# Layer 3 of a four-layer convolution net: who copies halo rows, how VectorE's side work begins and ends, and in which order pixels come back

## The chip, the core and the metric

The kernel runs on one core of a Trainium2 chip, in one launch. The metric is the device time in microseconds (us), as the median of several executions. The engines are named as in the profile: PE is TensorE's matmul, PEld its loading of weights, DVE is VectorE, ACT is ScalarE, POOL is GpSimd, and SP is the engine that issues most transfers.

## The reference

An input x of 4 images, 48 channels and 256 x 256 pixels, in f32, goes through four layers of the form x = x + f(groupnorm(x)). Layer 0 is a gated depthwise block with a frequency filter at its end; layers 1 and 2 are recurrent scans down, up, right and left through the image. Layer 3, the one that changes, computes this:

```python
y = einsum('oc,bchw->bohw', w_in, x)            # 48 -> 288 channels
yp = y in patches of 8 x 8
f = rfft2(yp) * fft_mask[None]                  # a real mask per channel and frequency
y = irfft2(f) put back as an image
y = depthwise 3 x 3 convolution(y, w_dw)        # padding 1
x1, x2 = split(y, 2, axis=1)                    # 144 channels each
g = gelu(x1) * x2
return einsum('oc,bchw->bohw', w_out, g)        # 144 -> 48 channels
```

## The kernel before

The four layers run one after the other. Layer 3 (line 716 on) handles the images in two pairs, and each pair in strips of 8 rows: 32 steps with rows and one short tail step that ends the last row, so 66 steps in all. A step is named (pair, strip) in the code.

**The stages of a step.** `fetch` (line 801) loads the raw rows through SP. `normed` (L818) applies the group norm on ScalarE, in four instructions, into `u`. `turned` transposes it (L830 on PE, copied by ACT in L834), and `waves` takes the patches to frequencies (L844, copied by ACT in L845 into `xf`, which shares its buffer with `u`). `spectrum` is run 16 times: TensorE mixes the channels (L855, tile `pz`), and VectorE multiplies by the mask on the way out of PSUM (L857 and L861). `pixels` brings one group of channels back to pixels, 16 matmuls (L886, tile `pp`) and two copies by ACT (L890), into a tile `z_` with two halo rows above and a halo column on either side.

**The five groups.** A pair has two images of 288 channels. The first 128 channels of x1 and of x2 are a0 and a1 for the first image and b0 and b1 for the second; the last 16 of each, for both images, are m, on 64 partitions. `order` lists them as a0, a1, b0, b1, m, and `back(step, k)` brings back group k.

**Who convolves.** TensorE convolves a0, a1 and m, with a diagonal 32 x 32 matrix for each of the nine taps (`taps`, L903, tile `pd`). Two generators, `lane(0)` and `lane(1)`, each own half of the array's rows; a tap of one lane is eight matmuls of the program. A lane takes m first where the strip's parity is its own, and then a0 and a1; at the end `gate` (L917, L918) applies gelu to x1 on ACT and multiplies by x2 on DVE, into the single buffers `g_a` and `g_m`. VectorE convolves b0 and b1 by itself (`side`, line 924): the first tap is an ACT instruction (L941) that starts an accumulator `acc`, in two halves of four rows; the eight other taps are 16 DVE instructions (L943). After b0's taps, ACT applies gelu to the whole accumulator (L947), and after b1's taps two DVE products (L950) end the unit.

**The end of a step.** `mixed` projects 144 channels to 48 on TensorE (L962 from VectorE's product, L971 from the gated buffers; tile `po`), adds the raw rows on DVE (L984), and issues the stores on SP (L991). It runs one step late: `store(steps[n - 1])` stands in step n. A lane may gate step n only when the store of step n - 1 has been put in the order.

**What sets the order.** The order of TensorE's and VectorE's instructions in this layer is the order in which the program is written out (a manual schedule for these two engines); ScalarE's and GpSimd's instructions are put in order by the framework's scheduler. `in_turns` (line 427) does the writing. It takes turns: each lane gives one tap; then pieces of `work()` (each a condition, a cost in us, an action) go out as the credit that the taps earn allows; then VectorE's `side` is advanced by as much time as has been spent, up to 4 us ahead. A piece whose condition isn't met holds up the pieces behind it. All PSUM tiles of this layer come from one pool of four.

**Halo rows.** Before a group's new pixels are written, the last two rows of the strip before are copied to rows 0 and 1 of the same tile: on GpSimd for a0, a1, b0 and b1 (L879), and on ScalarE for m (L877), whose two strips lie in different halves of the partitions.

## Time and profile before

| what | us |
|---|---|
| median of 3 executions (14871.17 to 14875.96) | 14873.32 |
| the profiled execution's own time | 14874.17 |
| its span, from the first to the last instruction | 14872.4 |
| PE busy in the span | 13297.2 (89%) |
| DVE busy | 7342.2 (49%) |
| ACT busy | 3320.0 (22%) |
| POOL busy | 2818.1 (19%) |
| layer 3, from its first to its last step's first spectrum | 9349 to 14757 |

The profile is of one execution. Its page gives the busy time of each engine, and the granted clock of TensorE in 40 slices. The trace answers with more: groups of instructions by line (count, busy time, mean length of one, the idle time before them and what ended it), the waits (who waited for whom: total, times, longest), the chain of work that ended last in order of time, the timeline, and windows (for a stretch of time: the busy time of PE, PEld, DVE, ACT and POOL with their instructions, the granted clock of TensorE, the share and the rate of the DMA). Times in the last two are counted from the span's start. Within layer 3 a tap of `L903` stands in the trace as 16 matmuls, two for each of the program's.

### The profile page before, as it was taken

To read this page: it belongs to the slowest core of one execution; us is meant where nothing else is said; L and a number is where in the kernel's file an instruction comes from. 1 tells how busy PE (TensorE), PEld (TensorE's weight loads), DVE (VectorE), ACT (ScalarE), POOL (GpSimd) and SP (SyncE) were. 2 spreads that over 40 slices of the span, in tenths; PEclk is the share of its full clock that TensorE was granted. 3 is DMA by queue.
4 is the path that set the end of the run, shared out by engine and by line. 5 is a ranking of instruction groups with operands and counts; after the bars stand their busy time and mean duration, and the time that the engine had idled before them with its cause. 6 is when DMAs were issued, how large, how long until landed. Compare 5 with 4: busy or idle time off the path is not lost.

```text
span 14872.4 us, 340743 instructions
## 1 busy us (share of the span) xinstructions
PE 13297.2 (89%) x155976; PEld 8329.4 (56%) x155976; DVE 7342.2 (49%) x13291; ACT 3320.0 (22%) x3110; POOL 2818.1 (19%) x1227
## 2 busy tenths in 40 slices
PE   3999999998999898889999978788888888888888
PEld 1444444445777676667767756444444444444444
DVE  5333333333333334433333445666666666666666
ACT  1222222222223000012330000233233323333322
POOL 0000000000000004410000144223222222322322
PEclk9999999999999999999999988899999989999999
DMA  7222222214755876767567676100100110011010
GB/s 161 48 52 47 49 51 47 49 46 95 153 136 155 159 151 165 183 139 148 144 157 157 133 186 158 28 19 19 23 19 19 23 19 19 19 23 19 19 23 17
DMA packets 1168810, 1219.21 MB, mean 82 GB/s; under 512 B 1025941, under 2 KB 1030541, under 8 KB 1106509
## 3 DMA queue, kind: packets, MB, share of 16 engines
q1 hardware_dynamic: 1069260, 649.62, 22.2%
q0 software_dynamic: 87488, 445.55, 10.7%
q10 hardware_dynamic: 10624, 102.24, 3.5%
q8 instruction: 1224, 20.05, 0.6%
q14 instruction: 214, 1.75, 0.0%
HBM read 699.84 MB, written 497.42 MB: 81 GB/s over the span
## 4 chain that ended last, share of the span: by engine, by line
PE 73%; DVE 15%; DMA 6%; ACT 2%; issue 2%; SPq 1%; POOL 1%; ACTq 0%; DVEq 0%; POOLq 0%
PE acc L502 32%; PE pd L270 13%; DVE acc L943 13%; PE pd L903 7%; PE pp L886 5%; PE pz L855 4%; PE ph L245 3%; DMA blk<-x 3%; PE po L971 2%; PE po L355 2%; PE po L962 2%; DMA x<-blk 1%; PE pf L333 1%; PE py L302 1%; DMA gx<-in_x 1%
## 5 line engine op out<-in xcount | busy, mean ns | idle before, releaser
L502 PE MATMUL acc<-line,w_down 96*96 96x256 f32 x12240 | 2650.5, 379 | 41.7 <-DMA in<-x 23.3
L943 DVE SCALAR_TENSOR_TENSOR acc<-z_b,wd,acc 128x1024 f32<-128x1024 f32 (+1 forms) x2080 | 2481.1, 1264 | 396.6 <-ACT acc L941 395.3
L502 PEld LDWEIGHTS acc<-line,w_down 96*96 96x96 f32 x12240 | 1996.0, 163 | 695.5 <-issue 42.4
L879 POOL COPY z_b<-z_b 128x512 f32<-128x512 f32 x128 | 1470.2, 11486 | 3096.1 <-DVE acc L943 3053.8
L886 PE MATMUL pp<-c_idft,z 128*128 128x128 f32 x10240 | 1374.7, 298 | 645.4 <-ACT xf L845 558.8
L886 PEld LDWEIGHTS pp<-c_idft,z 128*128 128x128 f32 x10240 | 1304.4, 194 | 925.9 <-ACT xf L845 613.4
L270 PE MATMUL pd<-main,diag 32*32 32x512 f32 x36864 | 1670.5, 599 | 32.8 <-issue 32.5
L903 PE MATMUL pd<-z_a,diag 32*32 32x512 f32 x37152 | 1589.0, 619 | 105.9 <-DVE g_m L918 93.9
L502 PE MATMUL acc<-line,w_left 96*96 96x256 f32 x6120 | 1362.7, 386 | 251.3 <-DVE line L685 251.3
L502 PE MATMUL acc<-line,w_right 96*96 96x256 f32 x6120 | 1335.1, 380 | 104.9 <-DVE line L646 40.9
L502 PEld LDWEIGHTS acc<-line,w_left 96*96 96x96 f32 x6120 | 1016.9, 166 | 596.7 <-DVE line L685 257.3
L502 PEld LDWEIGHTS acc<-line,w_right 96*96 96x96 f32 x6120 | 1002.1, 164 | 437.9 <-DVE line L646 42.8
L857 DVE TENSOR_TENSOR z<-pz,mask 128x512 f32<-128x512 f32 x1024 | 702.3, 686 | 590.3 <-PE pz L855 588.6
L270 PEld LDWEIGHTS pd<-main,diag 32*32 32x32 f32 x36864 | 594.2, 103 | 656.4 <-issue 536.4
L270 PE MATMUL pd<-rest,diag 32*32 32x512 f32 x18432 | 936.6, 597 | 22.9 <-issue 22.9
L646 DVE SCALAR_TENSOR_TENSOR line<-acc,b_right,in 96x256 f32<-96x256 f32 x1020 | 489.4, 480 | 882.2 <-PE acc L502 838.1
L565 DVE TENSOR_TENSOR line<-acc,in 96x256 f32<-96x256 f32 x1020 | 429.1, 421 | 927.3 <-PE acc L502 912.6
L605 DVE SCALAR_TENSOR_TENSOR line<-acc,b_down,in 96x256 f32<-96x256 f32 x992 | 476.1, 480 | 808.5 <-PE acc L502 808.5
L695 POOL TENSOR_TENSOR blk<-blk,line 96x1024 f32<-96x1024 f32 x248 | 705.4, 2873 | 867.7 <-DVE line L685 449.5
L903 PEld LDWEIGHTS pd<-z_a,diag 32*32 32x32 f32 x37152 | 415.1, 105 | 622.3 <-issue 352.4
L102 ACT ACTIVATE nrm<-nrm 96x2 f32<-96x2 f32 (+1 forms) x4 | 0.8, 204 | 3336.5 <-DVE nrm L101 3336.5
L685 DVE SCALAR_TENSOR_TENSOR line<-acc,b_left,in 96x256 f32<-96x256 f32 x992 | 475.7, 480 | 529.8 <-PE acc L502 529.8
(141 smaller groups left out, 12104.8 us busy)
## 6 DMA issues: line engine op xcount, KB each, us to landing
blk<-x ACTq DMA_DIRECT2D x64, 1536.0 KB, 23.6
in<-x SPq DMA_DIRECT2D x248, 384.0 KB, 11.0
dn<-line POOLq DMA_DIRECT2D x124, 768.0 KB, 9.7
rt<-line POOLq DMA_DIRECT2D x124, 768.0 KB, 9.8
in<-rt SPq DMA_DIRECT2D x124, 768.0 KB, 7.7
in<-dn SPq DMA_DIRECT2D x120, 768.0 KB, 5.5
in<-up SPq DMA_DIRECT2D x240, 384.0 KB, 11.1
up<-blk POOLq DMA_DIRECT2D x56, 1536.0 KB, 23.9
```

The lines of the kernel that those rows point to most:

```text
L270: nc.tensor.matmul(pd[32 * j : 32 * j + 32, i], diag[s, img // 2, t, :], z[s, R2 * j + t // 3 : R2 * j + t // 3 + R2, t % 3 : t % 3 + W], ...
L502: self.nc.tensor.matmul(acc, w[:, t, :], carry[:, :, t : t + m], start=(t == 0), stop=(t == 2))
L605: nc.vector.scalar_tensor_tensor(inner(line), acc, bd, new[p][r], ALU.add, ALU.add)
L646: nc.vector.scalar_tensor_tensor(blocks(inner(line)), blocks(acc), br, new, ALU.add, ALU.add)
L685: nc.vector.scalar_tensor_tensor(inner(line), acc, bl, new[p][r], ALU.add, ALU.add)
L695: (nc.vector if w0 == 0 else nc.gpsimd).tensor_tensor(part, part, inner(ln[p][:, f::2])[..., lo:hi].rearrange("p w i h -> p i h w"), ALU.add)
L855: nc.tensor.matmul(pz[:, b, 0 : 2 * HD], xf[s, q, :], wi[s, :], start=True, stop=True)
L857: nc.vector.tensor_tensor(z[:, q, 0 : 2 * n].rearrange("p (b c) -> p b c", b=2), pz[:, :, 0:n], mask[:, :, 0:n].to_broadcast([128, 2, n]), ...
L879: nc.gpsimd.tensor_copy(t[:, 0:2, 1 : W + 1], above[:, RB : RB + 2, 1 : W + 1])
L886: nc.tensor.matmul(pp[0:n, q // 4, :, q % 4 * PW : (q % 4 + 1) * PW], z[:, q0 + q, k * NM : k * NM + n], self.idft, start=True, stop=True,)
L903: nc.tensor.matmul(pd[32 * j : 32 * j + 32, i, 0:n, :], diag[s, 2 if g == "m" else half, t, :], zt[g][s, R2 * j + t // 3 : R2 * j + t // 3 ...
L943: nc.vector.scalar_tensor_tensor(acc[:, r:r1], z, w, acc[:, r:r1], ALU.mult, ALU.add)
```

## The change

Four things change, all but the first lines in layer 3.

1. `pixels`: the halo copies of a0, a1, b0 and b1 are written for ScalarE instead of GpSimd, like that of m.
2. VectorE's side work is cut in units (one for each step and half) that `aside` writes out. A unit's first taps on ScalarE (`start`) are written up to five taps before the unit ahead of it ends, if its pixels are there. What ends a unit is put off: the gelu of b0 by four of the following taps, the products of b1 by two each. The condition for `mixed` is now that the products have been written (`full`).
3. `work`: pixels come back in the order b0, m, a0, a1, b1 (before: b0, b1, m, a0, a1), the store of the step before comes after them all, and the next step's normalization and transposes stand ahead of b0. The lanes take a ahead of m.
4. `in_turns`: the side may be 2.5 us ahead instead of 4.0, up to 20 turns of a side that has nothing to give are passed over when nothing else moved, and the costs that steer it are changed (0.31 us a row instead of 0.28, 3.1 for two spectra instead of 2.1).

```diff
@@ in_turns
-            ahead = max(min(ahead + spent, 4.0), -4.0)
+            ahead, idle = max(min(ahead + spent, 2.5), -4.0), 0
             while ahead > 0 or not moved:
                 cost = next(side, None)
-                if not cost:
+                if cost:
+                    ahead, moved = ahead - cost, 1
+                elif cost is None or moved or idle > 20:
                     break
-                ahead, moved = ahead - cost, 1
+                else:
+                    idle += 1
             assert moved or not lanes
+
+    def aside(self, units):
+        later, begun = [], set()
+
+        def tick():
+            if later:
+                later[0][0] -= 1
+            while later and later[0][0] <= 0:
+                _, cost, work = later.pop(0)
+                work()
+                if cost:
+                    yield cost
+
+        def begin(k):
+            if k < len(units) and k not in begun and units[k][0]():
+                begun.add(k)
+                units[k][1]()
+
+        for k, (_, _, taps, last) in enumerate(units):
+            wait = 0 if k in begun else 2
+            while wait:
+                begin(k)
+                wait -= k in begun
+                yield from tick()
+                yield 0.0
+            for i, (cost, tap) in enumerate(taps):
+                if i >= len(taps) - 5:
+                    begin(k + 1)
+                tap()
+                yield cost
+                yield from tick()
+            later += [list(e) for e in last]
+        while later:
+            yield from tick()
+            yield 0.0
@@ pixels
-                elif g == "m":
+                else:
                     nc.scalar.copy(t[:, 0:2, 1 : W + 1], above[:, RB : RB + 2, 1 : W + 1])
-                else:
-                    nc.gpsimd.tensor_copy(t[:, 0:2, 1 : W + 1], above[:, RB : RB + 2, 1 : W + 1])
@@ side, now unit
+            def unit(step, half):
+                g, rows, made = f"b{half}", 1 if tail(step) else RB, []
+                parts = [(r, min(rows, r + RB // 2)) for r in range(0, rows, RB // 2)]
+                cost = [0.05 + 0.31 * (r1 - r) for r, r1 in parts]
...
+                def start():
+                    acc = mid.tile([128, RB, W], F32, name=f"acc{half}", tag=f"acc{half}", bufs=2 - half)
...
+                def curve():
+                    nc.scalar.activation(made[0][:, 0:rows], made[0][:, 0:rows], AF.Gelu)
+                    whole[step] = made
...
+                taps = [(c, lambda t=t, rs=rs: tap(t, *rs)) for t in range(1, 9) for rs, c in zip(parts, cost)]
+                if half == 0:
+                    last = [(4, 0.0, curve)]
+                else:
+                    last = [(2, c, lambda rs=rs: product(*rs)) for rs, c in zip(parts, cost)]
+                return lambda: (step, g) in ready, start, taps, last
@@ lane
-                    for img in (("m",) if step[1] % 2 == l else ()) + ("a",):
+                    for img in ("a",) + (("m",) if step[1] % 2 == l else ()):
@@ work
-                        yield always, 2.2, both(*[lambda q=q + i: spectrum(state["xf"], q) for i in range(2)]), 2.1
+                        yield always, 2.2, both(*[lambda q=q + i: spectrum(state["xf"], q) for i in range(2)]), 3.1
...
                     if not tail(step):
                         yield from spectra()
-                    yield back(step, 2)
                     if ahead:
                         state["u"] = normed(nxt)
                         turn, wave = front(nxt)
                         yield turn
-                    yield back(step, 3)
+                    yield back(step, 2)
                     if ahead:
                         yield wave
                     yield back(step, 4)
+                    yield back(step, 0)
+                    yield back(step, 1)
+                    yield back(step, 3)
                     if n:
                         yield store(steps[n - 1])
                     if later is not None and not tail(later):
                         fetch(later)
-                    yield back(step, 0)
-                    yield back(step, 1)
                 yield store(steps[-1])
 
-            self.in_turns([lane(0), lane(1)], work(), 1.12, side())
+            self.in_turns([lane(0), lane(1)], work(), 1.12, self.aside([unit(s, k) for s in steps for k in range(2)]))
```

## The prediction

> **What bounds the kernel now.** I read the page first: the strip of slices puts layer 3 in the last 15 of 40 (9349 to 14872 us), with TensorE at 8 tenths. Then the waits of that stretch:

> ```profile
> POOL z_b L879 <- DVE acc L943: 3053.8, 125, 56.0
> ACT acc L947 <- DVE acc L943: 634.9, 66, 10.1
> PE pp L886 <- ACT xf L845: 558.8, 60, 9.4
> DVE acc L943 <- ACT acc L941: 395.3, 64, 6.3
> PE pd L903 <- DVE g_m L918: 93.9, 31, 4.8
> ```

> TensorE stands 9.4 us in each of 60 steps for ScalarE's copy L845. That copy is queued behind the gelu L947, which waits 10.1 us for VectorE's last b0 tap. The chain of waits in order of time shows it for one step:

> ```profile
> 13669.97 1.25 ACT acc L941
> 13671.31 16.90 DVE acc L943 x15
> 13689.25 1.29 DVE acc L943
> 13690.57 1.91 ACT acc L947
> 13693.43 6.22 PE pp L886 x32
> ```

> So a serial path (first tap, 16 taps, gelu, xf) sets the step. The 3054 us of GpSimd's wait are cover, not cost: it waits for a source to become free, long before b0's next pixels.

> The windows show a second cost. Rows: two whole steps, the stall of the second, its half-clock time, and another half-clock time. Columns: the stretch and its length; busy PE, PEld, DVE, ACT, POOL with their instructions; granted clock; DMA share; GB/s.

> ```profile
> 13562.67:13733.34 170.67, 145.34 (x2106) 83.73 (x2097) 117.43 (x154) 53.09 (x54) 48.94 (x8) 0.93 0.11 20
> 13684.04:13693.43 9.39, 0.01 (x1) 0.00 (x0) 9.39 (x9) 2.86 (x3) 9.39 (x1) 0.73 0.00 0
> 13688.37:13698.61 10.24, 5.17 (x25) 5.18 (x25) 6.95 (x6) 4.74 (x4) 7.99 (x2) 0.50 0.00 0
> 13729.33:13732.75 3.42, 2.89 (x56) 1.04 (x64) 0.47 (x1) 0.00 (x0) 0.35 (x1) 0.50 0.00 0
> ```

> The clock is 0.50 for 10.24 us around the stall's end and 3.4 us after a shorter one. The pixel group takes 6.22 us there, 3.84 elsewhere. In two steps (170.67 us) that loses about 5.4 us (2.4 + 1.2 + 1.8), and stalls take 25.1 (2 x 9.39, 3.6, 1.8, 2 x 0.5); 140 us are work.

> [...] half-clock pieces are multiples of 3.41 us. Sorting layer 3's windows by TensorE's busy share, it halved after shares up to 0.4-0.5 and never above 0.52; no restore came below 0.85. [...] The z_b copy takes 11486 ns, z_a's 616. VectorE isn't hurt: tap starts are 1.196 us apart with such a copy running and without.

> **The change, part by part.** Each of 56 steps (4 to 31 of each pair of images) of the changed program has one and the same instruction order, so one step can be walked.

> *Halo copies.* Four 128x512 copies a step leave GpSimd. ScalarE gets them at about 0.62 us each (z_m's row L877: 619 ns), 2.5 us on an engine busy 31%. In order they are new waits: z_b1's halo waits for the ninth b1 tap, done about 46.8 us in the walk below, and ScalarE reaches it at 47.7, with z_a1's copies behind it. Cover 1 us, nothing charged; late by x, it costs at most x less 7 us, since those pixels come at 53. Removing the copies gains nothing: they were hidden.

> *Begin and end overlapped.* The first taps of b1 come before b0's taps end, so VectorE's 6.3 us a step before L943 goes. The gelu now follows xf on ScalarE and its taps are over by then: the 9.4 us stall goes, with the half clock behind it (about 2.1 us a step). That is 60 x 9.4 = 560 us plus 60 x 2.1 = 126 us at most.

> *New order.* What was hidden is not any more. Prices, from the timeline: tap 1.20, spectrum multiply 0.74 start to start, z copy 0.95, gelu 1.8; TensorE 1.07 a two-lane tap, 0.89 a one-lane tap, 3.77 for 16 pixel matmuls, 1.17 for two spectra, 8.03 for the projection.

> ```profile
> 11025.33 2.74 DVE L984 TENSOR_TENSOR xo<-po,raw 112x256 f32<-112x256 f32 x8 [6.49 <-PE po L971]
> 11027.99 13.23 DVE L943 SCALAR_TENSOR_TENSOR acc<-z_b,wd,acc 128x1024 f32<-128x1024 f32 x11
> 11063.42 2.93 ACT L818 ACTIVATE u<-raw,scp 112x512 f32<-112x512 f32 x4
> ```

> Zero is the projection's end. TensorE does two two-lane taps and one m tap (3.15) and one spectrum (3.75). The second spectrum needs a PSUM tile that the product g_a frees, and VectorE has the residual (0.14 to 2.80), then four b0 taps (7.61), then g_a (8.81) in its order. **New stall A: 5.1 us.** Then three pairs of spectra and four pairs of lone m taps take TensorE to 20.15. Eight spectra follow with no taps between: VectorE paces them (8 x 0.74 + 0.6 for g_m, to 27.4), TensorE's last ends at 25.1. The next step's normalization, which waits for it, takes 2.93; before, pixels and taps covered that. **Stall B: 3.0.** Transposes, b0 pixels and transform (1.8 + 3.77 + 3.68) end at 37.3. VectorE's last seven b0 taps end at 35.9 and let ScalarE write z_b0; it then has eleven instructions in a row (four copies, gelu, two m copies, two first taps, two z_a0 copies), 11.7 us, to 47.7. TensorE's m and a0 pixels end at 44.85. **Stall C: 2.8.** Then 3 taps, pixels, 8 taps, pixels, 5 taps, projection: 3.35 + 3.77 + 8.7 + 3.77 + 5.49 + 8.03 = 33.1, to 80.8.

> So 80.8 us a step at full clock, against 165.3 / 2 = 82.6 before: gone are 12.5 us of stalls, new are 10.9 and some at the paced spectra; the work is about 1.6 us less, with fewer switches between kinds.

> *DMAs.* SP issues a step's four stores and two loads of raw rows as before, both at the projection's end. A load lands in 5.3 us (median) and the normalization reads it some 25 us after the projection now, 38 before: nothing charged, and without that cover its landing time would lengthen B.

> *Half clock.* A, 5.1 us, always leaves a window under 0.46 busy; by where the windows fall the loss is 1.5 to 3.2 us, mean about 2.1. B with the thin spectra before it does so too (1.5 to 3.2), but ScalarE's chain starts from VectorE at 36.0 and needs the transform only at 38.8, so 1.45 us are covered: 0.7 charged. [...] Step: 80.8 + 2.1 + 0.7 = 83.6 us (49 windows for two steps are 83.63).

> *Ends of the pairs.* With b1 last, at a pair's last step 16 b1 taps (19.2 us) stand between the tail's pixels and the projection while TensorE waits. The same walk gives 125 us for the interval of 112.5, and 133 for the last 115: +12 and +18.

> Sum: the first spectra of before are 86.07 us apart (60 intervals; 86.7 in the first pair, 85.5 in the second). 56 x (86.07 - 83.6) = 138 saved, 30 lost: 108 net. The other early steps I take as even. The profiled execution took 14874.2 us (span 14872.4), 0.9 over the median 14873.3; from the median: 14765.

> **The rivals.** *R1: larger gain.* Stall A is shorter or the clock isn't halved there: about 81.5 us a step, 56 x 4.57 - 30 = 226 saved, 14647; I place it at 14670. For it: the 1.8 us stall of before didn't halve the clock. [...]

> *R2: no change.* The new stalls and their half clock equal the old: 85.3 us a step (25 windows), 56 x 0.77 - 30 = 13 saved, 14860. For it: the loop of before sits on whole windows (170.67 = 50 of them), and may settle on a worse one.

> *R3: slower.* One mechanism: the half clock after stall A. If two windows after A stay half, because one-lane m taps and spectra don't count as busy, TensorE runs at half speed from 8.9 for 11.2 us, which do 5.6 us of work: 5.6 lost instead of 2.1, 87.1 a step: 56 x -1.03 - 30 = 88 lost, 14961. It decides from 85.5 us a step on, a loss of 4.0 there. For it: TensorE is on the path throughout that stretch. Against: five lone m taps took 4.45 us, undisturbed, in 31 of the steps before.

> *R4: it does not do what it says.* ScalarE's order is decided by the scheduler; but in the built order gelu stands after xf, so here only a scheduling surprise elsewhere is left: as R2 in time, 14870.

> **How the numbers follow.** Forecast 0.53 (own range 14715 to 14840: 1 us a step in the walk is 56 us), larger gain 0.16, no change 0.14, slower 0.15, R4 0.02. A measurement can tell about 0.2% (30 us). Faster 0.53 x 0.98 + 0.16 = 0.68; same 0.15 (most of R2 and R4); slower 0.17 (R3, the rest). From 14675 to 14900 leaves out half of R1 and most of R3: 2 in 10.

> **What would show it.** PE pp <- ACT xf gone from the waits, and DVE acc <- ACT acc near zero. A new TensorE wait of about 5 us a step in pz for DVE g_a (A), 3 us in pt for ACT u (B), up to 3 in pd for ACT z_a (C). VectorE idle some 18 us a step before xo. Clock still about 0.92-0.95. Layer 3's first spectra 83.6 us apart; GpSimd near idle in it. I am wrong if the clock is near 1.0 or under 0.9 there, if z_b1's halo copy makes ScalarE wait, or if A isn't there.

## The result, and the profile after

The changed kernel takes **15381.89 us** (15378.28 to 15386.19) where the kernel before takes 14872.24 in the same session: a ratio of 1.0344 (95% interval 1.0326 to 1.0362). It is 3.4% slower. The prediction was 14765, faster.

The waits of layer 3 in the kernel after, from 9340 us to its end (who waited for whom: us in total, times, longest):

```profile
ACT z_b L918 <- DVE acc L980: 1944.0, 69, 32.4
DVE xo L1033 <- PE po L1020: 1287.0, 66, 21.4
PE pz L896 <- DVE g_a L957: 273.6, 56, 4.9
PE pt L871 <- ACT u L859: 161.4, 124, 2.4
...
DVE acc L980 <- ACT acc L974: 18.5, 2, 10.4
```

TensorE's waits are much as forecast. Its wait for xf (558.8 us) is gone, and VectorE's wait for the first taps went from 395.3 to 18.5. Stall A is there (`pz` for `g_a`: 273.6 / 56 = 4.9 us), and so is B (`pt` for `u`: 2.33 us and, one transpose later, another 0.26 to 0.39 in most steps). VectorE is idle some 20 us before `xo`. TensorE stands idle less than before, and yet the kernel is slower. So the time isn't in a wait, and the waits can't show it. The groups of TensorE can. First the kernel before, then the kernel after, in layer 3 (busy us, mean ns of one, idle before):

```profile
L855 PE MATMUL pz<-wi,xf 48*128 48x288 f32 x4096 | 658.3, 440 | 0.9 <-DVE g_m L918 0.6
L903 PE MATMUL pd<-z_m,diag 32*32 32x512 f32 x9216 | 581.0, 597 | 0.4
```

```profile
L896 PE MATMUL pz<-wi,xf 48*128 48x288 f32 x4096 | 1007.2, 647 | 284.3 <-DVE g_a L957 273.6 <-DVE z L902 10.6
L942 PE MATMUL pd<-z_m,diag 32*32 32x512 f32 x9216 | 980.9, 968 | 3.9 <-DVE xo L1033 3.3 <-DVE z L902 0.5
```

The same number of the same matmuls costs 349 us more in the spectra and 400 us more in the m taps: 749 us of busy time, more than the 510 us by which the spans differ. The page's strip of the granted clock says why:

```profile
PE   3999999998998998899989887999999989999998
PEclk9999999999999998899999998888888888888888
```

Layer 3 (from the 25th slice on) runs at 8 tenths throughout, with a busy TensorE above it. The windows of one step (from 13519.75 us) show where. Rows: the whole step; stall A; the half-clock stretch around and after it; the stretch from stall A to stall B; stall B; the second half-clock stretch. Columns as before.

```profile
13519.75:13614.10 94.35, 85.99 (x1038) 51.36 (x1035) 57.64 (x75) 28.82 (x31) 0.00 (x0) 0.80 0.07 16
13520.51:13525.40 4.89, 0.01 (x1) 0.01 (x2) 4.89 (x6) 0.00 (x0) 0.00 (x0) 0.81 0.89 224
13523.55:13554.27 30.72, 28.88 (x184) 11.46 (x186) 15.42 (x32) 1.22 (x2) 0.00 (x0) 0.50 0.07 9
13525.40:13555.06 29.66, 29.66 (x188) 11.73 (x188) 14.36 (x32) 1.22 (x2) 0.00 (x0) 0.51 0.02 2
13555.06:13557.40 2.34, 0.01 (x2) 0.01 (x1) 2.34 (x6) 2.28 (x4) 0.00 (x0) 1.00 0.00 0
13557.65:13564.45 6.80, 6.41 (x33) 6.35 (x33) 6.80 (x6) 2.21 (x3) 0.00 (x0) 0.50 0.01 2
```

The chain of work shows the cause of the stall and what is behind it (start us, us, what):

```profile
13519.43 2.46 DVE acc L980 x3
...
13522.93 1.28 DVE acc L980
13524.21 1.14 DVE g_a L957
13525.39 1.33 PE pz L896 x4
13526.72 3.59 PE pd L942 x32
...
13547.75 7.34 PE pz L896 x32
13555.12 2.94 ACT u L859 x4
```

Four b0 taps stand on VectorE before `g_a`; TensorE waits for the PSUM tile that `g_a` frees; and then it goes on with spectra (48 rows of the array) and lone m taps (32 x 32 matmuls, one lane), at a clock of 0.51 (fourth row). Spectra and m taps alternate in the elided lines. The last eight spectra (`pz`, 7.34 us) have no taps between them, and it is within them, 0.79 us before stall B, that the clock comes back: in 56 steps the last of the nine windows held spectra alone.

### The profile page after: what moved, and what is told of

It is laid out like the page before. It is cut to its first block, busy times and chain, and to the rows that moved or that the text cites. A ratio compares the mean times of both kernels' runs of the same rounds, so it can differ in the third digit from the quotient of the medians.

```text
span 15382.2 us, 340406 instructions
## 1 busy us (share of the span) xinstructions
PE 14044.2 (91%) x155976; PEld 8841.3 (57%) x155976; DVE 7341.0 (48%) x13291; ACT 3455.8 (22%) x3366; POOL 1273.2 (8%) x971
## 4 chain that ended last, share of the span: by engine, by line
PE 82%; DMA 6%; ACT 5%; DVE 4%; issue 1%; POOL 1%; SPq 1%; ACTq 0%; DVEq 0%; POOLq 0%
PE acc L543 31%; PE pd L942 13%; PE pd L270 13%; PE pz L896 6%; PE pp L925 5%; PE ph L245 3%; DMA blk<-x 3%; DVE acc L980 2%; PE po L1020 2%; PE po L1011 2%; PE po L355 2%; DMA x<-blk 1%; PE pf L885 1%; PE pf L333 1%; PE py L302 1%
## 5 line engine op out<-in xcount | busy, mean ns | idle before, releaser
L980 DVE SCALAR_TENSOR_TENSOR acc<-z_b,wd,acc 128x1024 f32<-128x1024 f32 (+1 forms) x2080 | 2484.9, 1263 | 19.6 <-ACT acc L974 18.5
L942 PE MATMUL pd<-z_a,diag 32*32 32x512 f32 x37152 | 1375.4, 598 | 39.1 <-ACT z_a L929 35.3
L925 PEld LDWEIGHTS pp<-c_idft,z 128*128 128x128 f32 (+1 forms) x10240 | 1234.1, 191 | 131.8 <-issue 75.5
L925 PE MATMUL pp<-c_idft,z 128*128 128x128 f32 (+1 forms) x10240 | 1283.1, 287 | 0.2 <-ACT xt L875 0.2
L896 PE MATMUL pz<-wi,xf 48*128 48x288 f32 x4096 | 1007.2, 647 | 284.3 <-DVE g_a L957 273.6
L896 PEld LDWEIGHTS pz<-wi,xf 48*128 48x128 f32 x4096 | 574.1, 296 | 950.3 <-issue 442.6
L942 PE MATMUL pd<-z_m,diag 32*32 32x512 f32 x9288 | 989.4, 963 | 7.2 <-DVE xo L1033 6.5
L942 PEld LDWEIGHTS pd<-z_a,diag 32*32 32x32 f32 x37152 | 664.1, 103 | 566.1 <-issue 248.9
L1033 DVE TENSOR_TENSOR xo<-po,raw 112x256 f32<-112x256 f32 x512 | 175.6, 415 | 1287.0 <-PE po L1020 1287.0
```

The source lines that it names most:

```text
L896: nc.tensor.matmul(pz[:, b, 0 : 2 * HD], xf[s, q, :], wi[s, :], start=True, stop=True)
L925: nc.tensor.matmul(pp[0:n, q // 4, :, q % 4 * PW : (q % 4 + 1) * PW], z[:, q0 + q, k * NM : k * NM + n], self.idft, start=True, stop=True,)
L942: nc.tensor.matmul(pd[32 * j : 32 * j + 32, i, 0:n, :], diag[s, 2 if g == "m" else half, t, :], zt[g][s, R2 * j + t // 3 : R2 * j + t // 3 ...
L980: nc.vector.scalar_tensor_tensor(to, at(t, r, r1), wd[:, half, t : t + 1], to, ALU.mult, ALU.add)
```

## The experiments

After the result the theory (T in the expectations) was: stall A is as short as forecast, but *the work behind it is too thin to bring the clock back*, however busy TensorE is with it. Rivals: what restores the clock is the share of time in which TensorE is busy, as the prediction took it; the new order as such is what costs; the new limit and costs; the halo copies on ScalarE. All medians below are to be read beside 14862.75 (first four runs), 14861.9 (next four) and 14865.81 us (last two) for the kernel before in the same sessions.

**1. No b0 taps ahead of g_a.** One number of the changed kernel: the VectorE work charged for an output group. The four b0 taps go behind the spectra.

```diff
-                    return done, 8.2, go, 3.5
+                    return done, 8.2, go, 12.0
```

> The changed kernel with one number changed: the store's cost for VectorE is 12.0 instead of 3.5, so that no b0 taps are written between the residual and the two products g_a (in the changed kernel there are four; they move behind the spectra). Theory T (the clock): TensorE's 4.9 us wait for g_a halves the clock, and the lone m taps and spectra behind it keep the array too thinly used to get it back, for 30.7 us a step. Then this kernel loses the wait and the half clock of that stretch: a step goes from 94.7 to about 80, 56 x 14.7 = 820 us less, some 14560. Theory O (the new order is long whatever the clock does): only the wait goes, 4.9 us a step or less, and the b0 taps come back on the way to z_b0: 15110 to 15380. Theory H (ScalarE's halo copies set the step): about 15380.

Measured: 14441.22 us, ratio 0.9715 (0.97 to 0.9729), on T's side and somewhat lower than its figure. The waits for `g_a` are gone from TensorE's list. The windows show the same first stretch of a step (18 us from its start), the half-clock stretch after stall B, and the whole step:

```profile
12869.86:12887.74 17.88, 17.66 (x197) 7.29 (x192) 12.56 (x30) 0.60 (x1) 0.00 (x0) 1.00 0.35 73
12890.46:12897.29 6.83, 6.53 (x33) 6.53 (x34) 6.83 (x7) 2.67 (x4) 0.00 (x0) 0.50 0.00 0
12869.86:12948.14 78.28, 73.94 (x1053) 46.93 (x1048) 57.72 (x77) 28.88 (x31) 0.00 (x0) 0.96 0.10 21
```

All spectra with the same lone m taps now take 17.88 us at a clock of 1.00. The thin work is not slow by itself; *behind the stall* it takes 29.66 us at 0.51 (the changed kernel). Removing a stall of 4.9 us took 16.3 us off the step (94.74 to 78.44, means over both pairs).

**2. Dense work behind the stall.** The changed kernel with sixteen useless 128 x 128 matmuls, once a step, between the first spectra after stall A and the next ones. They compute nothing that is read.

```diff
+                def warm():
+                    t = ps_w.tile([128, 8, 128], F32, name="warm", tag="w")
+                    for q in range(16):
+                        nc.tensor.matmul(t[:, q % 8, :], self.idft, self.idft, start=True, stop=True)
...
+                        if q == 2:
+                            yield always, 0.0, warm, 0.0
```

> The changed kernel with useless work added: 16 full-size matmuls (128x128 by 128 columns, constants, into a PSUM tile that nobody reads) after the first pair of spectra of each step and the m taps behind it, just where the clock is half. Theory T: they fill one window, the clock comes back behind them, and 20 us of half-rate work run at full rate: plus 4 to 7.5 us, minus about 10 us a step, so FASTER than the changed kernel by 2 to 5 us a step, 15100 to 15280. Theories O and H: slower by at least the 3.8 us that such a group takes, 15600 or more.

Measured: 15089.76 us, ratio 1.0146 (1.0129 to 1.0163): with work *added*, 292 us faster than the changed kernel, as T has it (just below its range of 15100 to 15280). Windows: the thin work before the added group, the group, and the thin work after it up to the last group of spectra:

```profile
13341.80:13346.75 4.95, 4.93 (x37) 1.24 (x37) 2.56 (x5) 0.00 (x0) 0.00 (x0) 0.50 0.08 10
13346.68:13352.01 5.33, 5.33 (x42) 5.21 (x34) 0.00 (x0) 0.00 (x0) 0.00 (x0) 0.70 0.00 0
13351.94:13366.39 14.45, 14.33 (x153) 6.21 (x152) 10.35 (x25) 1.22 (x2) 0.00 (x0) 1.00 0.01 1
```

Stall A is unchanged (274.9 us, 57 times). The clock comes back inside the dense group (0.70 over it) and is 1.00 for the 14.45 us behind it.

**3. The halo copies alone undone.** The changed kernel with a0, a1, b0 and b1 copied by GpSimd.

```diff
-                else:
+                elif g == "m":
                     nc.scalar.copy(t[:, 0:2, 1 : W + 1], above[:, RB : RB + 2, 1 : W + 1])
+                else:
+                    nc.gpsimd.tensor_copy(t[:, 0:2, 1 : W + 1], above[:, RB : RB + 2, 1 : W + 1])
```

> The changed kernel with its first part undone: the halo copies of a0, a1, b0 and b1 are on GpSimd again. Theory T and theory O: nothing, 15382 within 40 us, as no copy is on the path. Theory H: faster by more than 100 us.

Measured: 15406.18 us, ratio 1.0365 (1.0349 to 1.038), 24 us above the changed kernel. With the rest of the change in place, the copies have no part in the loss.

**4. The units alone.** Part 2 of the change (units, `aside`, the condition `full`, the passed-over turns) on the kernel before: pixel and lane order, halo copies, limit 4.0 and the costs 0.28 and 2.1 are those of before. The diff against the changed kernel:

```diff
-            ahead, idle = max(min(ahead + spent, 2.5), -4.0), 0
+            ahead, idle = max(min(ahead + spent, 4.0), -4.0), 0
...
-                cost = [0.05 + 0.31 * (r1 - r) for r, r1 in parts]
+                cost = [0.05 + 0.28 * (r1 - r) for r, r1 in parts]
...
-                    for img in ("a",) + (("m",) if step[1] % 2 == l else ()):
+                    for img in (("m",) if step[1] % 2 == l else ()) + ("a",):
...
+                    yield back(step, 2)
...
-                    yield back(step, 2)
+                    yield back(step, 3)
...
-                    yield back(step, 0)
-                    yield back(step, 1)
-                    yield back(step, 3)
...
+                    yield back(step, 0)
+                    yield back(step, 1)
```

> The second part alone: VectorE's units begin and end overlapped, everything else (halo copies on GpSimd, order of the pixels, lanes with m first, costs and the limit of 4.0) as before. Theory T: the 9.4 us wait for xf goes with the half clock behind it, nothing thin follows a stall: about 11.5 us a step less than before, 60 x 11.5 = 690, some 14180 to 14350. Rival (the overlapped units themselves cost, by what they queue on ScalarE): 14873 or more.

Measured: **14249.55 us**, ratio 0.9587 (0.9573 to 0.9602), faster than both kernels by 4% and more. The longest of TensorE's waits left in it:

```profile
PE pd L944 <- DVE g_m L959: 122.7, 30, 4.9
PE pp L927 <- DVE g_m L959: 55.9, 30, 2.2
```

So the part that removes the serial path is worth about 613 us by itself, and the other parts took more than that away again.

**5. Thin work behind the stall.** The kernel of experiment 2 with one line changed: the same sixteen matmuls at the same place, with as many streamed columns, on 32 x 32 of the array.

```diff
-                        nc.tensor.matmul(t[:, q % 8, :], self.idft, self.idft, start=True, stop=True)
+                        nc.tensor.matmul(t[0:32, q % 8, :], self.idft[0:32, 0:32], self.idft[0:32, :], start=True, stop=True)
```

> The same sixteen useless matmuls at the same place as in the run with dense work after stall A, with the same number of streamed columns, but each on 32 rows by 32 columns of the array instead of 128 by 128. Theory T (after a stall the clock comes back only when enough of the array is streaming; a busy TensorE is not enough): the group does not restore the clock, it runs at half speed itself (about 5.3 us) and everything up to the transforms stays halved; the step grows from 94.7 us by about 5.3, to about 100; 15382 + 62 x 5.3 = about 15710 us, between 15650 and 15770. Rival S (what restores the clock is the share of time in which TensorE is busy, as the prediction took it): the thin group does what the dense one did, about 15090 us, step near 88.8.

Measured: 15759.73 us, ratio 1.0608 (1.0592 to 1.0623). The same three stretches as in experiment 2:

```profile
13794.09:13799.02 4.93, 4.93 (x38) 1.54 (x39) 2.54 (x5) 0.00 (x0) 0.00 (x0) 0.50 0.13 14
13798.77:13805.80 7.03, 7.03 (x42) 5.41 (x33) 0.00 (x0) 0.00 (x0) 0.00 (x0) 0.50 0.00 0
13805.73:13830.57 24.84, 24.84 (x153) 10.58 (x152) 11.87 (x27) 1.22 (x2) 0.00 (x0) 0.52 0.00 1
```

In both kernels TensorE is busy without a gap through the added group. On the whole array it restores the clock, and the 153 matmul records behind it take 14.45 us at 1.00; on 32 x 32 it doesn't, and they take 24.84 at 0.52. That excludes the busy share as what decides.

**6. Order, lanes and halo copies as before, limit and costs as changed.**

```diff
+                elif g == "m":
...
+                    nc.gpsimd.tensor_copy(t[:, 0:2, 1 : W + 1], above[:, RB : RB + 2, 1 : W + 1])
...
+                    for img in (("m",) if step[1] % 2 == l else ()) + ("a",):
...
+                    yield back(step, 2)
...
+                    yield back(step, 3)
...
+                    yield back(step, 0)
+                    yield back(step, 1)
```

> The changed kernel with the pixel order, the lane order and the halo copies of before; the units, the limit 2.5 and the costs 0.31 and 3.1 stay. Theory T: no b0 taps stand before g_a at the spectra's start, so stall A is gone; but with the new costs both tap products stand late on VectorE (nine taps, g_a, eight taps, then two taps, product, two taps, product), and the output matmuls that need the first product come after about 25 us of TensorE work: a stall of 4 to 7 us in front of po, with one-lane m taps behind it. Step 69.9 us of full-clock work + about 6 + about 8 for thin work at half clock = 80 to 85; 14500 to 14900 us. Rival O (the new pixel order itself is what costs): with the order undone this is the units-alone kernel with other limits, 14250 +-60 us. Rival L (the new limit and costs are what costs, whatever the order): above 15000 us.

Measured: 14647.34 us, ratio 0.986 (0.9846 to 0.9875): inside T's range, step 81.9 us, but **not by T's stall**. TensorE hardly ever waits at `po`; it waits 3.3 to 3.5 us a step for m's pixels:

```profile
PE pd L944 <- ACT z_m L931: 197.2, 59, 3.8
```

ScalarE's second copy of m's pixels stands behind two copies into `z_b` that wait for VectorE's last b1 taps (its timeline):

```profile
13067.12 1.02 ACT L931 COPY z_m<-pp 64x1024 f32<-64x1024 f32 x1 [0.88 <-PE pp L927]
13070.24 1.95 ACT L931 COPY z_b<-pp 128x1024 f32<-128x1024 f32 x2 [2.10 <-DVE acc L982]
13072.21 1.02 ACT L931 COPY z_m<-pp 64x1024 f32<-64x1024 f32 x1
```

Lone m taps follow, and the clock is half for 13.7 us (0.51 from 13072 to 13086). Against the units alone, the new limit and costs are worth +398 us with the old order: they move the taps, and with them which ScalarE instruction is in front.

**7. The units with the halo copies on ScalarE.** Experiment 4, with the copies of part 1.

```diff
-                elif g == "m":
+                else:
                     nc.scalar.copy(t[:, 0:2, 1 : W + 1], above[:, RB : RB + 2, 1 : W + 1])
-                else:
-                    nc.gpsimd.tensor_copy(t[:, 0:2, 1 : W + 1], above[:, RB : RB + 2, 1 : W + 1])
```

> The units alone (14249.55 us) plus the halo copies of z_a and z_b on ScalarE instead of GpSimd; order, lanes, limit and costs as before. Theory T: the copies are off the path on either engine; 14200 to 14270 us. Rival H (the copies on ScalarE lie on the path that releases the taps, 192 copies of about 0.6 us): up to 60 us slower, or, if GpSimd's slow copies held the taps in the units-alone kernel, up to 100 us faster.

Measured: 14622.4 us, ratio 0.9843 (0.9827 to 0.986). Both theories miss: it is 373 us slower than the units alone, where the same edit changed nothing in experiment 3. Its waits in layer 3, and its chain of work at one place:

```profile
PE pd L942 <- ACT z_a L929: 178.8, 32, 6.0
PE pp L925 <- ACT xf L886: 136.9, 60, 7.7
```

```profile
13125.82 10.77 DVE acc L980 x9
...
13136.61 0.62 ACT z_b L918
13137.23 0.94 ACT z_a L929
...
13138.21 4.05 PE pd L942 x60
```

The copy takes 0.62 us, but it may only start when VectorE's last tap has read the rows. On GpSimd it waited there (1595.9 us in the units alone, 65 times), and nothing that TensorE waited for was behind it. On ScalarE the copies that TensorE needs (`z_a`, and `xf` in the other place) are behind it: TensorE stands 6.0 us, and the run's granted clock is 0.957 where that of the units alone is 0.971. In the changed kernel ScalarE stands at such a copy for even longer, 32.4 us in most steps (`ACT z_b L918` in the first list of waits). What stands behind it there is m's gelu, whose taps come from TensorE only later (in the step above the copy starts at 13540.44 and the gelu at 13547.86, after a further wait of 6.80 us for the taps), so nothing that TensorE needs was held up.

**8. The order alone.** The kernel before with the new pixel order and lane order; no units, old limit and costs, GpSimd copies.

```diff
-                    for img in (("m",) if step[1] % 2 == l else ()) + ("a",):
+                    for img in ("a",) + (("m",) if step[1] % 2 == l else ()):
...
-                    yield back(step, 2)
...
-                    yield back(step, 3)
+                    yield back(step, 2)
...
+                    yield back(step, 0)
+                    yield back(step, 1)
+                    yield back(step, 3)
...
-                    yield back(step, 0)
-                    yield back(step, 1)
```

> The kernel before with only the new pixel order and the new lane order (a before m); no units, limit 4.0, costs 0.28 and 2.1, halo on GpSimd. Theory T: the first taps of b0 wait for ScalarE's start of the accumulator, five of them stand on VectorE before g_a, and the second half of the forward transform waits for g_a about 6 us; behind it lie one-lane m taps, at half clock (about 7 us lost) until the transforms restore it: 69.9 + 2.3 + 6 + 7 + 4 = about 89 us a step, 15060 us, between 14850 and 15300. Rival O2 (the order by itself is an improvement, since it takes the wait for xf away: 9.3 us a step, and the loss is the units' alone): 14300 to 14600 us.

Measured: 15251.86 us, ratio 1.0264 (1.0249 to 1.0279). The sum is right, its parts only half. The stall at the forward transform is 4.76 us (6 expected), and a second one of 4.53, not expected, stands at the first spectra, where VectorE's taps are ahead of the mask product. The timeline of TensorE behind the first of them:

```profile
13510.51 3.75 PE L844 MATMUL pf<-c_dft_p,xt 128*112 128x128 f32 x16 [4.76 <-DVE g_a L918]
13514.20 6.49 PE L903 MATMUL pd<-z_m,diag 32*32 32x512 f32 x112
```

The transform is dense and pays the half clock alone (0.50 from 13508.10 to 13514.80; 3.75 us where 16 records took 2.00 ahead of the stall); the 112 records of lone m taps behind it run at 58 ns each, with the clock at 0.95 (61 ns in experiment 1 at 1.00, 114 in the changed kernel at 0.50). The expectation had charged these m taps 7 us. So T holds where its own application failed: in this run the dense work *first* behind the stall spared the thin work the half clock. Behind the second stall the spectra alternate with taps of both lanes, and there the half clock lasts two or three windows (28 and 30 of 58 steps), not nine.

**9 and 10. A version that beats both.** The units alone, with one number, so that VectorE reaches `g_m` sooner (8.0 in the first, 12.0 in the second):

```diff
-                    return done, 8.2, go, 3.5
+                    return done, 8.2, go, 8.0
```

> The units alone (14249.55 us) with one number changed: the work that VectorE is charged for an output group is 8.0 instead of 3.5, so that nine or ten b1 taps stand between xo and g_m instead of ten and fourteen, and the rest go among the spectra. Theory T: the stall of 4.9 us in front of g_m in every other step (and its half-clock window, 1.7 us lost) is gone, and the 1.8 us one in the other; the taps moved among the spectra cost about 0.4 us each, up to four a step. About 2 to 3 us a step less: 14060 to 14150 us. Rival V (VectorE is the bound among the spectra, and the moved taps cost what the stall did): 14200 to 14300 us.

> As the run before, with 12.0 instead of 8.0: four and seven b1 taps between xo and g_m, up to four more among the spectra and the rest late. Theory T: no stall at g_m in either kind of step, as with 8.0; no further gain from g_m; 14050 to 14200 us. Rival V: slower than with 8.0 by 0.4 us for each tap moved further, so 14250 to 14350 us.

Measured: **14042.42 us** with 8.0, ratio 0.9443 (0.9427 to 0.9459), and 14209.76 with 12.0, ratio 0.9556 (0.9542 to 0.957). With 8.0, two steps in the windows:

```profile
12550.64:12695.40 144.76, 141.67 (x2100) 78.54 (x2096) 116.89 (x155) 53.51 (x54) 17.95 (x8) 1.00 0.12 24
```

TensorE is busy for 141.67 of 144.76 us at a clock of 1.00; half-clock time in layer 3 is 53 us, against 851.5 before. The gain is a little over T's price (75.75 to 72.34, so 3.4 us a step, where 2 to 3 were expected). With 12.0 three steps of four take 71 to 73 us, but the taps put off pile up, and in each fourth (84.8 us) the old serial path is back, in ScalarE's timeline:

```profile
12923.59 1.01 ACT L886 COPY xf<-pf 112x1024 f32<-112x1024 f32 x1 [0.34 <-PE pf L885]
12935.17 1.91 ACT L989 ACTIVATE acc<-acc 128x2048 f32<-128x2048 f32 x1 [10.57 <-DVE acc L982]
12936.99 0.99 ACT L886 COPY xf<-pf 112x1024 f32<-112x1024 f32 x1
```

The gelu waits 10.57 us for VectorE with the second xf copy behind it. The run ends just above T's range and below rival V's; neither foresaw this wait.

## Why the prediction was wrong

**The step that failed is "Half clock".** It charged 2.1 us for stall A and 0.7 for B, the author's estimates. Measured: the spectra and m taps behind A take 29.66 us, and in experiment 1, at full clock, the same instructions take about 17.1 (17.88 less the 0.8 that lie ahead of the stall): 12.5 us lost. Behind B, transposes and b0's pixels take 3.06 + 5.44 us where the units alone need 1.75 + 3.84: 2.9. Together 15.4 us a step instead of 2.8, times some 56 steps about 700 us: more than the whole miss (15382 - 14765 = 617).

**Why it failed.** The prediction had sorted windows by TensorE's busy share and found that no restore came below 0.85. That is so, but it is only half of the question. The same trace of before has 149 windows that stayed at half clock (from layer 3's first to its last step's first spectrum), and in 26 of them TensorE was busy for 0.85 or more: they were there to be counted. In the trace after there are 432 of 506. A bound taken from the restores says what is needed, not what is enough. In the step above, 29.66 us of work without a gap ran at 0.51.

**The rival R3** named this mechanism and gave it 0.15. Its argument, that a TensorE busy with one-lane m taps and spectra need not get the clock back, was right (388 of 388 such windows, last section); its size, two more windows and 5.6 us, was not: spectra mixed with lone m taps stayed at half clock until the last eight spectra, which stand alone, so it is nine windows (in 56 steps). What spoke against it, five lone m taps that ran undisturbed before, was no evidence: there the clock was full already (1.00: 80 records in 4.52 us, 56 ns each, against 114 ns behind stall A: 32 in 3.66). In experiment 1 the same thin work left a full clock full (1.00 over 17.88 us).

**What was right, and how near.** *Stall A*: 4.89 us (5.1), for the reason given. *Stall B*: 2.33 and 0.39 (3.0 together). *Stall C*: 0.46 to 0.75 (2.8); ScalarE's eleven instructions were counted right, but with the clock halved TensorE came later, and with experiment 1's shorter half-clock time it is 1.07 to 1.41. No half clock follows it in the step above (1.00 from 13564.48 to 13614.10). *VectorE idle before xo*: 19.9 to 21.4 us (18). *The wait for xf* and the late first taps: gone. *The walk at full clock*: 94.74 - 15.4 = 79.3 us a step, of which the three stalls are about 8.2, so about 71 of work (predicted 80.8, 10.9 and 69.9); experiment 1 steps at 78.44. *Halo copies*: z_b1's copy finds its taps done, as walked. The copy that waits is z_b0's, 32.4 us for the ninth b0 tap, which the walk didn't have; TensorE doesn't wait for it, and undoing the copies gave nothing, as charged. *Ends of the pairs*: the change of pairs takes 196.1 us in two intervals against 191.8, +4.3 instead of +12, and the last step to the end 156.2 against 115.0, +41 instead of +18; together 45 against 30.

**Of its conditions for being wrong** one was met: the clock in layer 3 is 0.82, "under 0.9".

**The parts of the change.** With the others as before, the units are worth -613 us (experiment 4) and the order +390 (8). They don't add up: with the order, the new limit and the halo copies on top of the units, it is about +1130 (the two costs included). What each does depends on which instruction then stands in front of VectorE's or ScalarE's queue. The numbers of the kernel's own bookkeeping matter as much: the charge for an output group (3.5, 8.0 or 12.0) was worth 40 to 940 us, the limit and the two costs together 398.

**What stays open.** Which of the limit and the two costs puts the four taps before `g_a` in the changed kernel was not separated. What in the use of the array the clock answers to (its rows, its columns, both) is open too: experiments 2 and 5 show only that sixteen matmuls on 128 x 128 restored it (1.00 behind them) and on 32 x 32 didn't (0.52).

## What to carry to other kernels

When a change adds a stall to TensorE, ask what the first work behind it is. Here the dense transform behind a stall of 4.76 us (experiment 8) had the clock back as the lone m taps behind it began (0.95 over them), while thin work (spectra on 48 rows, m taps on 32 x 32, one lane) behind a stall of 4.89 us paid the half clock for nine windows: 12.5 us, more than twice the stall itself. That loss was in no wait; it showed in the mean length of one matmul (the spectra: 440 ns before, 647 after) and in the clock of the layer (0.92 before, 0.82 after). And before giving a small copy to ScalarE, ask what it waits for and what is behind it: in experiment 7 its own 0.62 us were the least of it, with 178.8 us of TensorE's waits for the `z_a` copies behind it.

## What the runs showed of the hardware

The two directions of the clock differed in these runs. At full clock, spectra mixed with lone m taps kept it (experiment 1: 1.00 over 17.88 us). At half clock the same mixture never brought it back: in the trace after, all 388 windows of 3.413 us that held it or m taps alone, with TensorE busy for 0.85 or more, were followed by another at half clock. So in these runs the mixture kept whichever clock it found. Spectra alone did either: of the windows at half clock that held nothing else, TensorE again busy for 0.85 or more, 56 were followed by full clock and 13 by half. Sixteen 128 x 128 matmuls brought it back (experiment 2: 1.00 behind them), sixteen on 32 x 32 didn't (5: 0.52). The counts of windows are of one trace; that the share of the array in use is what decides is the author's estimate from them, and wasn't tested by itself.

Stalls shorter than a window halved the clock too. In layer 3 of the changed kernel, each of the 57 gaps of TensorE of 2.2 to 2.5 us that began at full clock (B's first part) was followed by half clock within 3.42 us of its end, and so was B in the step of experiment 1 above (0.50 over 6.83 us). In experiment 8 stalls of 1.25 and 0.39 us in front of the same transposes, with one transpose between them, halved it in 60 steps of 60, while a single 1.78 us in experiment 4 and 1.33 in experiment 9 did not (none of 14, none of 15). In layer 3 of the kernel before, counted in the same way, all 78 gaps over 3.413 us were followed by half clock, and 19 of the 47 from 1.6 to 3.413 us: of the 30 under 1.95 us 6 were, so that the prediction's single 1.8 us stall was too little to go by.
